# Five buffers for the last image's convolution blocks, in a kernel ordered by a planner

## The chip, the cores and the metric

The kernel runs on one core of one Trainium2 chip. The metric is the device time of one launch in microseconds (us). Five engines work side by side, each through its own instructions in order: TensorE (PE, with its weight loads shown apart as PEld), VectorE (DVE), ScalarE (ACT), GpSimd (POOL) and SyncE (SP), which here issues nearly all DMA transfers.

## The reference

Four images of 128 channels, 128 x 128 pixels, all float32, go through two residual layers.

```python
# layer 0, both halves of `_L0_conv_ref` have the same tokens and weights
x = x + block(gn(x)) + block(gn(x) transposed) transposed
#   block: t = ln0(tokens); t = t + silu(ln1(t)) @ W_out
#          w = ln2(t) @ W_whiten; k = relu(w @ W_key) ** 2
#          t = t + sigmoid(w @ W_recep) * (k @ W_value)
# layer 1
h = gn(x)
avg = h.mean(axis=(2, 3))
out = conv3x3(h, weight[0], padding=1) + bias[0]      # the gate always picks expert 0
se = sigmoid(relu(avg @ se_w1.T) @ se_w2.T)
x = x + out * se
```

The block works on each pixel (token) alone, so its transposed second half equals the first and is computed once with a factor of two. `gn` takes its mean and variance over a group of four channels of a whole image. So layer 1 of an image can't start before layer 0 of all its pixels is done: this is what shapes the end of the kernel.

## The kernel before, in words

**Work.** Layer 0 (`layer0(g)`) goes in steps `g` of 1024 pixels, 16 an image, 64 in all. A step's results are added into the block of 16 rows in a buffer with the tag `x`; after two steps the block is stored to memory (`xo`, L1100) in `spill[b]`, and statistics for the second `gn` are gathered on the way (`bx`, L1093).

Layer 1 is `conv(k, at)`, one block of 16 rows at a time, eight an image, 32 in all. It loads 18 rows (the block and a row above and below) from `spill[b]` into a buffer with the tag `xc` (L1119). The 3 x 3 convolution is computed by rows in a fast scheme that makes four rows of output from six products instead of twelve:

- VectorE forms row sums `p`, `q` (L1167, L1168) and `p2`, `q2` (L1174, L1175), tag `vt`, and from them and the rows the six inputs `v1`, `v2`, `v3`, `v4`, `v0`, `v5` (L1170, L1173, L1176, L1177, L1178 with L1179, L1180 with L1181). Their tag is `v`, with four buffers; for the last image `put` takes `h` instead, with six buffers.
- TensorE makes six products (`product(i)`, L1191 to L1193, three taps each) in the order 1, 2, 3, 4, 0, 5 with the kernels `T["uw", b, i]`, tag `uw`.
- ScalarE moves products 1 and 3 out of their banks (`e`, L1206 and L1214); VectorE forms `a`, `e1` (`ab`, L1210, L1211), `c`, `e3` (`cd`, L1218, L1219) and six operations named `y` (L1220 to L1227), which write the four output rows over rows 1 to 16 of the block's own buffer. L1225 needs product 0, L1227 product 5.
- The buffer is then stored to the output (L1237; for the last block in four parts, L1232). Only then is it free for another block's load.

Before an image's first product stands a chain of small steps, `conv_setup`: aggregate the statistics (L551), group means on TensorE (L554), variances, a root on GpSimd (L571), the squeeze-and-excite factors (L578 to L601), and the scaling of the six kernels on VectorE (L620, L626). The kernels are fetched from memory by `uw` (L633).

**Order.** Nothing is ordered by hand. Each operation is handed to a `Plan` by `op`, with its engine, an assumed cost, what it reads, writes and allocates, and a priority: the step or block it belongs to plus a number by its name from the table `SHIFT` (a low priority goes first). `Plan.order` simulates the five engines: whenever one is free it looks at the operations that are ready soonest, within `LOOK` of the first, and takes the one with the lowest priority (plus `HASTE` times its delay). `ROOM` says how many buffers each tag has; an operation that allocates is ready only when a buffer of its tag is free in the plan. The instructions are then issued in that order. So the convolution blocks of images 0 to 2 fall between the layer 0 steps of the image that follows, while the last image's eight blocks have nothing left to be mixed with. `TAIL_BANKS` gives their products six banks.

For the steps below, `x` has three buffers, `xc` two, `vt` four, `uw` nine. SP issues every load and store in plan order, and waits at the head of its queue for what the next one needs.

Of the kernel before, what the change touches and what calls it, by code (L numbers as in the profile page):

```python
# [13 lines left out]
P = 128  # L14
CH = 512
SUB = CH // P
PAIR = 2
BLK_ROWS = 16
# [2 lines left out]

BEGIN = {"ACT": 12.0, "POOL": 8.0, "PE": 8.0, "DVE": 0.5, "SP": 0.5}
SHIFT = {
    "R": -74.134, "Rc": 16.802, "Rm": -33.629, "S": 24.028, "T": -69.812, "Tz": -48.318,
    "W": -20.432, "ab": 34.928, "att": 0.537, "b": 24.437, "bn0": -1.666, "bn1": -17.948,
    "bn2": -13.51, "bx": 36.779, "c": 7.347, "cag": 14.439, "cav": -29.375, "cd": -89.85,
    "cp": -49.531, "cp1": -1.659, "cpm": -25.194, "cpr": -67.859, "cpv": -61.584, "cre": 67.032,
    "crt": -69.645, "csg": -13.711, "csp": -35.976, "cth": -17.338, "cve": 53.588, "e": 5.36,
    "e0": 16.432, "e1": -68.352, "e2": -62.698, "edge": 61.941, "fw": 14.812, "g": -11.425,
    "gag": -8.273, "gnb": -12.519, "gpm": -0.463, "gpv": -28.192, "grt": 16.489, "gsp": -8.03,  # L30
    "gve": -25.322, "in": 31.37, "in0": 114.307, "kv": 3.481, "late": 10.91, "m0": 22.359,
    "m1": -99.072, "o": -46.745, "pk": 3.203, "pq": -6.546, "pr": 2.671, "q": -82.946,
    "raw": -57.415, "rc": -6.49, "re": -98.005, "silu": -105.386, "sq": -108.331, "sqd": -40.877,
    "t": 9.446, "tD": -51.982, "tR": 23.098, "tW": -6.661, "th": -63.552, "tt": 94.047, "u": 21.426,
    "us": -20.273, "ut": 67.121, "ut2": -0.423, "uw": -43.592, "v": 45.831, "w": 114.443,
    "w0": 42.845, "w1": -39.745, "w2": -14.719, "x": 74.139, "x1": -55.714, "xc": -4.177,
    "xd": -0.904, "xf": -62.031, "xo": -5.878, "xs": -72.633, "y": 1.545, "z": 17.673, "zD": 12.117,
    "zR": 15.727, "zW": -3.804,
}
SQUARES = (("DDAA", "DDAA"), ("AAAA", "AAAA"))  # L40
TAIL_BANKS = ("Bkv", "Btr", "Btr", "Bh", "Bconv", "Bh")
CONV_AT, CONV_STEP = 2.0, 2.0
LOOK = {'PE': 0, 'DVE': 0.07, 'ACT': 0.05, 'POOL': 0, 'SP': 0.058}
HASTE = 16.739
SQUARES_AT = 17
ROOM = dict(
    x=3, xd=2, xs=2, ut=3, t=7, z=2, y=2, zd=2, zc=2, td=2, tt=2, R=2, y2=2, h=6, r=2, xc=2, vt=4, v=4,
    yt=4, uw=9, Bh=3, Bkv=1, Btr=2, Bconv=2, st=6, rs=6, nb=4, four=2, rrow=2, rd=2, zs=2, ts=2,
)
READ_AT = 3  # L50
BACKLOG = 2.189
FIRST_U_ON_DVE = (2, 3)


# [187 lines left out]
def conv_preact_kernel(  # L242
# [20 lines left out]
    nc = tc.nc  # L263
    B, C, H, W = x.shape
# [7 lines left out]
    PER = BLK // CH  # L272
# [8 lines left out]
    ps = ctx.enter_context(tc.tile_pool(name="ps", bufs=2, space=bass.MemoryType.PSUM))  # L281

    SHAPE = dict(
        x=[P, BLK_ROWS, W], xd=[P, SUB, CH], xs=[P, PAIR * CH], ut=[P, SUB, C], t=[P, SUB, C],
        z=[P, SUB, C], y=[P, CH], y2=[P, CH], h=[P, CH], r=[P, CH],
        xc=[P, BLK_ROWS + 2, W], vt=[P, Q, W], v=[P, Q, W], yt=[P, Q, W], uw=[P, 3, P],
        st=[P, N, 3], rs=[P, N], nb=[P, N], four=[P, 4, N], rrow=[P, 4 * N],
# [6 lines left out]
    T = {}  # L294

    def make(t, tag):
        pool = ps if tag[0] == "B" else sb
        T[t] = pool.tile(SHAPE[tag], F32, tag=tag, name=t[0], bufs=ROOM[tag])
        return T[t]
# [22 lines left out]
    late = []  # L322
# [51 lines left out]
    for i, (name, by) in enumerate((("g1", C**0.5), ("b1", 1.0), ("g2", C**0.5), ("b2", 1.0), ("cb", 1.0))):  # L374
        t = const.tile([P, 1], F32, tag=name, name=name)
# [4 lines left out]
    for name, row, by in (("g0", row0[0], 2 * C**0.5), ("b0", row0[1], 2.0)):  # L380
        pr = bank("prow")
        nc.tensor.matmul(pr[:, :C], ones, row, start=True, stop=True)
        t = const.tile([P, C], F32, tag=name, name=name)
# [8 lines left out]
    for src, n, dst, bias, by in ((wkt, HID, wk_s, kbias, 1.0), (wrt, P, wr_s, rbias, 0.5)):  # L392
        pw = bank("pw")
        nc.tensor.matmul(pw[:, :n], ww, src, start=True, stop=True)
        raw, raw2 = staged("raw", n), staged("raw2", HID)
# [17 lines left out]
    spill = [dram.tile([P, H, W], F32, tag=f"xo{b}", name=f"xo{b}", bufs=1) for b in range(B)]  # L413
# [5 lines left out]
    V, A, G, E, D = "DVE", "ACT", "POOL", "PE", "SP"  # L419
    TINY = (0.16, 0.2)  # L420
    READ, WRITE = (0, 0.85), (0, 0.4)

    def op(name, eng, cost, prio, emit, reads=(), writes=(), new=(), port=False, bus=0.0):
        return plan.op(name, eng, cost, prio + SHIFT.get(name, 0.0), emit, reads, writes, new, port, bus)

    def rows_of(k):
        b, kb = divmod(k, NBLK)
        return x[b, :, kb * BLK_ROWS : (kb + 1) * BLK_ROWS, :]

    def chunk_rows(t, r):  # L430
        return t[:, r :: PER, :]

    def one_input(b, i, src):
        if b not in st0:
# [300 lines left out]
    def layer0(g):  # L735
        b, p = divmod(g, NP)
        k = b * NBLK + p * PAIR // PER
        xt, xd = ("x", k), ("xd", k)
        if p * PAIR % PER == 0:

            def load():
                nc.sync.dma_start(make(xt, "x"), rows_of(k))

            op("x", D, READ, g, load, (), [(xt, r) for r in range(PER)], [(xt, "x")], bus=3.05)
            load_turned(k)
            for q in range(SUB):

                on_dve = k == 0 and q in FIRST_U_ON_DVE

                def lay(q=q, on_dve=on_dve):  # L750
                    rs, nb = gn0[b]
                    scale, bias = rs[:, q : q + 1], nb[:, q : q + 1]
                    if on_dve:
                        nc.vector.tensor_scalar(T[xd][:, q], T[xd][:, q], scale, bias, ALU.mult, ALU.add)
                    else:
                        nc.scalar.activation(T[xd][:, q], T[xd][:, q], AF.Identity, bias=bias, scale=scale)

                op(
                    "u", V if on_dve else A, (0.61, 0.7) if on_dve else (0.705, 0.82), g, lay, [(("gn0", b), 0), *((xd, a) for a in range(SUB))],
                    [(xd, ("u", q))],  # L760
                )
# [117 lines left out]
        for h in range(PAIR):  # L879
            r = (p * PAIR + h) % PER  # L880
# [11 lines left out]
        for h in range(PAIR):  # L892
            t = ("t", g, h)
# [9 lines left out]
            on, cost = (V, (0.605, 0.685)) if GAIN_ON_DVE(g) else (G, (1.232, 1.272))  # L903
# [11 lines left out]
        for h in range(PAIR):  # L915
            t, z, zt, y, att = (("t", g, h), ("z", g, h), ("zt", g, h), ("y", g, h), ("att", g, h))
# [8 lines left out]
        for h in range(PAIR):  # L925
            t, z, zt, y, att = (("t", g, h), ("z", g, h), ("zt", g, h), ("y", g, h), ("att", g, h))
            if Z_BY_DMA(g):
                zc = ("zc", g)
# [33 lines left out]
        R = ("R", g)  # L962
# [25 lines left out]
        for h in range(PAIR):  # L988
            r = (p * PAIR + h) % PER
            t, y2 = ("t", g, h), ("y2", g, h)  # L990
            if T_BY_DMA(g):
                tt = ("tt", g)
                to_channels("t", t, ("td", g), tt, h)
        for h in range(PAIR):
            r = (p * PAIR + h) % PER
            t, y2 = ("t", g, h), ("y2", g, h)
            tt = ("tt", g) if T_BY_DMA(g) else ("ttp", g, h)
# [30 lines left out]
            for j in range(NH):  # L1028
                pk, hh = ("pk", g, h, j), ("h", g, h, j)
# [24 lines left out]
            pr, gate, kv = ("pr", g, h), ("r", g, h), ("kv", g, h)  # L1054
# [41 lines left out]
        if p * PAIR % PER == PER - PAIR:  # L1096
            kb = k % NBLK

            def store():
                nc.sync.dma_start(spill[b][:, kb * BLK_ROWS : (kb + 1) * BLK_ROWS, :], T[xt])  # L1100

            op("xo", D, WRITE, g, store, [(xt, r) for r in range(PER)], [(("xo", b), kb)], bus=3.1)

# [3 lines left out]
    def conv(k, at):  # L1107
        b, kb = divmod(k, NBLK)
        ending = b == B - 1
        gn = gn1[b]  # L1110
        xc = ("xc", k)
        first, last = kb == 0, kb == NBLK - 1
        lo, hi = max(0, kb * BLK_ROWS - 1), min(H, (kb + 1) * BLK_ROWS + 1)
        shift = lo - (kb * BLK_ROWS - 1)
        n = hi - lo
        parts = ("r0", 1, 2, 3, 4, "r17")

        def load():
            nc.sync.dma_start(make(xc, "xc")[:, shift : shift + n, :], spill[b][:, lo:hi, :])  # L1119

        near = [(("xo", b), i) for i in range(max(0, kb - 1), min(NBLK, kb + 2))]
        op("xc", D, READ, at, load, [*near, (("gv1", b), 0)], [(xc, s) for s in parts], [(xc, "xc")], bus=3.4)
        for edge, row, part in ((first, 0, "r0"), (last, BLK_ROWS + 1, "r17")):
            if edge:

# [10 lines left out]
        def units(s):  # L1136
            return [(xc, p) for p in {0: ("r0", 4), 5: (1, "r17")}.get(s, (s,))]

        def name_of(n):
            return (n, k)  # L1140
# [11 lines left out]
        def do(name, eng, cost, fn, reads=(), writes=(), new=(), port=False):  # L1152
            new = [(t, "h" if tag == "v" and ending else tag) for t, tag in new]
            op(name, eng, cost, at, fn, reads, writes, new, port)
# [2 lines left out]
        TWO = (0.605, 0.685)  # L1157

        def inner(name, tag, fn, rows_in=(), tiles_in=(), extra=(), cost=TWO, inplace=False):
            t = name_of(name.rstrip("ab") if name in ("v0a", "v0b", "v5a", "v5b") else name)  # L1160
            reads = [u for s in rows_in for u in units(s)] + [(name_of(i), 0) for i in tiles_in] + list(extra)
            do(
                "v" if tag == "v" else "pq", V, cost, fn, reads + ([(t, 0)] if inplace else []), [(t, 0)],
                () if inplace else [(t, tag)], True,
            )

        inner("p", "vt", lambda: stt(put("p", "vt"), rows(2), -4.0, rows(4), ALU.mult, ALU.add), (2, 4))  # L1167
        inner("q", "vt", lambda: stt(put("q", "vt"), rows(1), -4.0, rows(3), ALU.mult, ALU.add), (1, 3))  # L1168
# [140 lines left out]
```

## Time and profile before

| what | value |
|---|---|
| median of 3 runs | 1767.89 us (1765.37 to 1768.89) |
| the profiled execution, its own time | 1767.58 us |
| its span | 1765.8 us, 18695 instructions |
| granted TensorE clock, mean | 0.995 of full speed |
| busy: PE / DVE / ACT / POOL | 1698.4 / 1421.0 / 1295.7 / 1173.4 us |
| moved by DMA | 354.66 MB, mean 201 GB/s |

How to read it: busy time is what an engine's instructions cover, matmul ends being modelled. The number in brackets at the end of a line of the timeline is the idle time just ahead of the instruction, with what ended it. A wait for several things is put down to the one that came last. A matmul in float32 appears as two records (`x2`), and three taps make one product, so a block has 36 records on PE. An SPq line is the issue of a DMA, not its transfer.

### The profile page before, as it was taken

The numbers are of one execution on the slowest core, as the hardware profiler recorded it, in microseconds if no ns is written. First come the engines' busy times: TensorE is split into PE (matmuls) and PEld (weight loads), VectorE is DVE, ScalarE is ACT, GpSimd is POOL, SyncE is SP. The second block draws the span as 40 slices with busy tenths as digits, with TensorE's granted clock in tenths as the row PEclk, the third lists the DMA queues.
The fourth block names the chain that finished last, engine by engine and source line by source line (L and its number), as shares of the span: only waits on it lengthen the run. The fifth ranks groups of instructions, "written<-read, shape, count | busy, mean of one in ns | idle before, by whom it ended". The sixth has DMA issues, their size and how long they took to land.

```text
span 1765.8 us, 18695 instructions
## 1 busy us (share of the span) xinstructions
PE 1698.4 (96%) x4870; PEld 815.2 (46%) x4870; DVE 1421.0 (80%) x2619; ACT 1295.7 (73%) x2656; POOL 1173.4 (66%) x1085
## 2 busy tenths in 40 slices
PE   5899999999999999999999999999999999998898
PEld 2444445444444444444445454444444444443343
DVE  5898788799899876879898777898988766458776
ACT  1999898998998777888878869988897865430000
POOL 1778887888897777788887858969788753210000
PEclk9999999999999999999999999999999999999999
DMA  9456666576687877767867677566777664223232
GB/s 319 131 170 209 202 195 191 171 227 222 180 259 241 244 244 231 219 224 224 271 209 259 228 251 223 189 206 197 241 222 246 202 202 139 84 76 137 107 146 97
DMA packets 140170, 354.66 MB, mean 201 GB/s; under 512 B 19079, under 2 KB 78750, under 8 KB 122782
## 3 DMA queue, kind: packets, MB, share of 16 engines
q1 hardware_dynamic: 139472, 352.99, 62.7%
q8 instruction: 39, 0.64, 0.1%
q14 instruction: 69, 0.57, 0.1%
q10 hardware_dynamic: 590, 0.46, 0.1%
HBM read 230.31 MB, written 123.07 MB: 200 GB/s over the span
## 4 chain that ended last, share of the span: by engine, by line
PE 34%; POOL 6%; DVE 5%; ACT 3%; issue 1%; DMA 1%; SPq 0%; DVEq 0%; POOLq 0%
PE kv L1070 8%; PE pk L1032 7%; PE m L1191 5%; PE m L1193 5%; PE m L1192 5%; PE pr L1057 2%; PE att L953 1%; POOL rs L819 1%; POOL four L790 1%; POOL x L1025 1%; ACT t L838 1%; POOL t L907 1%; POOL x L1085 1%; ACT h L1037 1%; POOL t L910 1%
## 5 line engine op out<-in xcount | busy, mean ns | idle before, releaser
L1070 PE MATMUL kv<-h,wv 128*128 128x512 f32 x1024 | 526.5, 598 | 9.1 <-DVE h L1049 4.2
L1032 PE MATMUL pk<-y,wk_s 128*128 128x512 f32 x1024 | 484.2, 597 | 3.2 <-ACT h L1037 2.7
L1037 ACT ACTIVATE h<-pk,kbias 128x512 f32<-128x512 f32 x512 | 335.8, 681 | 92.9 <-PE pk L1032 84.8
L1032 PEld LDWEIGHTS pk<-y,wk_s 128*128 128x128 f32 x1024 | 190.0, 190 | 237.1 <-issue 173.1
L1070 PEld LDWEIGHTS kv<-h,wv 128*128 128x128 f32 x1024 | 183.2, 190 | 215.3 <-issue 166.3
L1043 ACT ACTIVATE h<-h 128x512 f32<-128x512 f32 x444 | 267.8, 628 | 2.6
L1085 POOL TENSOR_TENSOR x<-x,r 128x512 f32<-128x512 f32 x128 | 168.4, 1316 | 145.7 <-DVE r L1079 140.5
L819 POOL TENSOR_TENSOR rs<-rs,nhalf 128x8 f32<-128x8 f32 (+1 forms) x134 | 227.0, 1697 | 40.1 <-ACT rs L816 39.9
L838 ACT ACTIVATE z<-t,nb,rs 128x128 f32<-128x128 f32 x512 | 209.5, 490 | 19.0 <-POOL nb L824 18.7
L838 ACT ACTIVATE t<-ut,nb,rs 128x128 f32<-128x128 f32 x512 | 209.4, 488 | 16.9 <-DVE st L769 9.8
L1191 PE MATMUL m<-v,uw 128*128 128x512 f32 x384 | 198.4, 598 | 14.8 <-DVE v L1170 13.7
L769 DVE BATCH_NORM_STATS2 st<-t 128x6 f32<-128x256 f32 x512 | 187.4, 411 | 20.9 <-POOL t L910 20.7
L1193 PE MATMUL m<-v,uw 128*128 128x508 f32 x384 | 196.6, 594 | 0.0
L907 POOL TENSOR_TENSOR t<-t,g 128x512 f32<-128x512 f32 x124 | 160.8, 1300 | 53.7 <-ACT t L838 53.0
L1192 PE MATMUL m<-v,uw 128*128 128x508 f32 x384 | 196.5, 593 | 0.0
L1014 POOL TENSOR_TENSOR y<-tt,R 128x512 f32<-128x512 f32 x96 | 127.4, 1331 | 74.5 <-PE pk L1032 60.6
L1025 POOL TENSOR_TENSOR x<-tt,x 128x512 f32<-128x512 f32 x124 | 163.8, 1333 | 11.5 <-DMA tt<-ts 11.1
L910 POOL TENSOR_TENSOR t<-t,b 128x512 f32<-128x512 f32 x124 | 162.0, 1315 | 2.4
L953 PEld LDWEIGHTS att<-wo,y 128*128 128x128 f32 x1024 | 130.9, 192 | 57.2 <-issue 34.7
L953 PE MATMUL att<-wo,y 128*128 128x128 f32 x1024 | 133.9, 277 | 4.2 <-ACT y L946 2.3
L1062 ACT ACTIVATE r<-pr,rbias 128x512 f32<-128x512 f32 x128 | 87.2, 681 | 67.0 <-POOL x L1085 59.6
L1079 DVE SCALAR_TENSOR_TENSOR r<-r,kv 128x512 f32<-128x512 f32 x128 | 86.9, 679 | 61.1 <-PE kv L1070 59.4
(160 smaller groups left out, 2309.7 us busy)
## 6 DMA issues: line engine op xcount, KB each, us to landing
xd<-in_x SPq DMA_DIRECT2D x128, 256.0 KB
x<-in_x SPq DMA_DIRECT2D x32, 1024.0 KB
xo<-x SPq DMA_DIRECT2D x32, 1024.0 KB
R<-rd SPq DMA_DIRECT2D x63, 512.0 KB
ts<-td SPq DMA_DIRECT2D x248, 128.0 KB
tt<-ts SPq DMA_DIRECT2D x62, 512.0 KB
out<-xc SPq DMA_DIRECT2D x31, 1024.0 KB
xc<-xo SPq DMA_DIRECT2D x24, 1152.0 KB
```

What stands on the lines that cost most here:

```text
L769: nc.vector.bn_stats(st[:, i : i + 2, :].rearrange("p n f -> p (n f)"), two)
L819: nc.gpsimd.tensor_tensor(T[rs][:, part], T[rs][:, part], nhalf[:, :k], ALU.pow)
L838: nc.scalar.activation(dst[:, s, :], src[:, s, :], AF.Identity, bias=nb[:, i : i + 1], scale=rs[:, i : i + 1])
L953: nc.tensor.matmul(pa[:, ts(m, P)], T[y][:, ts(m, P)], wo2, start=True, stop=True)
L1032: nc.tensor.matmul(make(pk, "Bh"), wk_s[:, ts(j, P)], T[y2], start=True, stop=True)
L1037: nc.scalar.activation(make(hh, "h"), T[pk], AF.Relu, bias=kbias[:, j : j + 1])
L1043: nc.scalar.activation(T[hh], T[hh], AF.Square)
L1070: nc.tensor.matmul(T[kv], wv[:, j, :], T["h", g, h, j], start=(j == 0), stop=(j == NH - 1))
L1085: nc.gpsimd.tensor_tensor(xs, xs, T[gate].rearrange("p (a w) -> p a w", a=SUB), ALU.add)
L1191: nc.tensor.matmul(pc, u[:, 1], vv, start=True, stop=False)
L1192: nc.tensor.matmul(pc[:, :, 1:W], u[:, 0], vv[:, :, 0 : W - 1], start=False, stop=False)
L1193: nc.tensor.matmul(pc[:, :, 0 : W - 1], u[:, 2], vv[:, :, 1:W], start=False, stop=True)
```

## The change

- The blocks of the last image take their buffer from `TAIL_HOMES`: blocks 0, 1, 5 and 6 from `xc` as before, blocks 2, 3, 4 and 7 from `x`, whose three buffers belong to the finished layer 0 blocks. For this `x` gets 18 rows; layer 0 uses 16 of them.
- `vt` goes from four buffers to three, `uw` from nine to eight.
- In `inner`, new dependencies named `turned` let `p`, `q`, `v1`, `v2` of block k be planned only after `v1`, `v2` of block k - 1, and the other row sums (`p2`, `q2`) after the other inputs of block k - 1; an input `v` of either kind only after all inputs of block k - 1. All of these are VectorE instructions.
- `SHIFT`, `LOOK`, `HASTE` and `BACKLOG` have new values; `hot` gets an entry of its own. They change the order of all operations.

```diff
 SHIFT = {
...
-    "W": -20.432, "ab": 34.928, "att": 0.537, "b": 24.437, "bn0": -1.666, "bn1": -17.948,
...
-    "us": -20.273, "ut": 67.121, "ut2": -0.423, "uw": -43.592, "v": 45.831, "w": 114.443,
...
-    "xd": -0.904, "xf": -62.031, "xo": -5.878, "xs": -72.633, "y": 1.545, "z": 17.673, "zD": 12.117,
...
+    "ab": 37.315, "att": 1.644, "b": 31.731, "bn0": 11.794, "bn1": -17.35, "bn2": -15.592,
+    "bx": 49.609, "c": 7.82, "cag": 6.719, "cav": -18.068, "cd": -103.804, "cp": -37.768,
...
+    "hot": -13.329, "in": 26.361, "in0": 105.375, "kv": 3.816, "late": 12.753, "m0": 23.5,
+    "m1": -101.213, "o": -54.585, "pk": 3.497, "pq": -18.954, "pr": 3.288, "q": -106.007,
...
+    "u": 16.271, "us": -19.465, "ut": 67.807, "ut2": 9.337, "uw": -50.513, "v": 57.985, "w": 117.982,
...
+    "xf": -58.371, "xo": -10.863, "xs": -54.606, "y": 24.867, "z": 15.121, "zD": 21.243,
...
 }
+TAIL_HOMES = ("xc", "xc", "x", "x", "x", "xc", "xc", "x")
-LOOK = {'PE': 0, 'DVE': 0.07, 'ACT': 0.05, 'POOL': 0, 'SP': 0.058}
-HASTE = 16.739
+LOOK = {'PE': 0.018, 'DVE': 0.087, 'ACT': 0.048, 'POOL': 0.004, 'SP': 0.048}
+HASTE = 31.975
 ROOM = dict(
-    x=3, xd=2, xs=2, ut=3, t=7, z=2, y=2, zd=2, zc=2, td=2, tt=2, R=2, y2=2, h=6, r=2, xc=2, vt=4, v=4,
-    yt=4, uw=9, Bh=3, Bkv=1, Btr=2, Bconv=2, st=6, rs=6, nb=4, four=2, rrow=2, rd=2, zs=2, ts=2,
+    x=3, xd=2, xs=2, ut=3, t=7, z=2, y=2, zd=2, zc=2, td=2, tt=2, R=2, y2=2, h=6, r=2, xc=2, vt=3, v=4,
+    yt=4, uw=8, Bh=3, Bkv=1, Btr=2, Bconv=2, st=6, rs=6, nb=4, four=2, rrow=2, rd=2, zs=2, ts=2,
 )
-BACKLOG = 2.189
+BACKLOG = 1.96
...
-        x=[P, BLK_ROWS, W], xd=[P, SUB, CH], xs=[P, PAIR * CH], ut=[P, SUB, C], t=[P, SUB, C],
+        x=[P, BLK_ROWS + 2, W], xd=[P, SUB, CH], xs=[P, PAIR * CH], ut=[P, SUB, C], t=[P, SUB, C],
...
-        return t[:, r :: PER, :]
+        return t[:, r : BLK_ROWS : PER, :]
...
-                nc.sync.dma_start(make(xt, "x"), rows_of(k))
+                nc.sync.dma_start(make(xt, "x")[:, :BLK_ROWS, :], rows_of(k))
...
+        home = TAIL_HOMES[kb] if ending else "xc"
+
         def load():
-            nc.sync.dma_start(make(xc, "xc")[:, shift : shift + n, :], spill[b][:, lo:hi, :])
+            nc.sync.dma_start(make(xc, home)[:, shift : shift + n, :], spill[b][:, lo:hi, :])
...
         def inner(name, tag, fn, rows_in=(), tiles_in=(), extra=(), cost=TWO, inplace=False):
-            t = name_of(name.rstrip("ab") if name in ("v0a", "v0b", "v5a", "v5b") else name)
+            t = name_of(name[:2] if tag == "v" else name)
             reads = [u for s in rows_in for u in units(s)] + [(name_of(i), 0) for i in tiles_in] + list(extra)
+            writes = [(t, 0)]
+            half = "12" if name in ("p", "q", "v1", "v2") else "0345"
+            if tag == "v":
+                writes += [(("turned", k, half), name)]
+                reads += [(("turned", k - 1, hf), v) for hf in HALVES for v in HALVES[hf]]
+            else:
+                reads += [(("turned", k - 1, half), v) for v in HALVES[half]]
...
+        HALVES = {"12": ("v1", "v2"), "0345": ("v3", "v4", "v0a", "v0b", "v5a", "v5b")}
```

## The prediction

> **What bounds the kernel now.** I read the page's first part, then the busy time by stretch. Columns of the second fence: stretch, its length, busy us (and instructions) of PE, PEld, DVE, ACT, POOL, then granted clock, DMA share, GB/s.
>
> ```profile
> PE 1698.4 (96%) x4870; PEld 815.2 (46%) x4870; DVE 1421.0 (80%) x2619; ACT 1295.7 (73%) x2656; POOL 1173.4 (66%) x1085
> ```
>
> ```profile
> 0.00:88.00 88.00, 60.69 (x200) 32.61 (x201) 61.28 (x121) 51.10 (x122) 38.84 (x67) 0.98 0.72 226
> 88.00:330.00 242.00, 233.60 (x777) 118.24 (x776) 205.27 (x406) 222.87 (x466) 194.71 (x189) 1.00 0.63 194
> 330.00:1590.00 1260.00, 1249.84 (x3545) 597.98 (x3544) 1018.73 (x1864) 1009.96 (x2050) 937.20 (x829) 1.00 0.67 211
> 1590.00:1766.00 176.00, 154.25 (x352) 66.34 (x350) 135.73 (x230) 11.80 (x20) 2.64 (x2) 0.97 0.32 122
> ```
>
> TensorE is the bound. Its idle time is 27.3 us in the start, 8.4 up to 330, 10.2 in the 1260 us of the middle, and 21.7 in the last 176, where the last image is convolved. Of the middle there is little to be had; the tail is where the change acts. There I asked for TensorE's waits (1597 to 1766) and for the load queue's own (1540 to 1766): us in total, times, longest.
>
> ```profile
> PE m L1191 <- DVE v L1170: 13.7, 8, 3.2
> PE cpm L554 <- DVE mv L551: 2.1, 1, 2.1
> PE m L1191 <- DVE uw L626: 0.8, 1, 0.8
> ```
>
> ```profile
> SPq L1119 <- DMA out<-xc: 32.4, 9, 4.6
> ```
>
> TensorE waits eight times for v1 (L1170), the first of a block's six inputs; and each block's load (L1119) waits for an earlier block's store, since there are two `xc` buffers. One block in order of time (start, length, what, idle before it):
>
> ```profile
> 1659.02 0.34 SPq L1237 DMA_DIRECT2D out<-xc  x1
> ...
> 1662.82 0.32 SPq L1119 DMA_DIRECT2D xc<-xo  x1
> ...
> 1665.27 0.69 DVE L1210 TENSOR_TENSOR a<-m,e 128x512 f32<-128x512 f32 x1 [1.40 <-PE m L1193]
> ...
> 1667.83 0.69 DVE L1167 SCALAR_TENSOR_TENSOR p<-xc 128x512 f32<-128x512 f32 x1 [1.15 <-DMA xc<-xo]
> ...
> 1670.39 0.69 DVE L1218 TENSOR_TENSOR c<-m,e 128x512 f32<-128x512 f32 x1 [0.67 <-PE m L1193]
> ...
> 1675.44 0.69 DVE L1227 TENSOR_TENSOR xc<-m,e 128x512 f32<-128x512 f32 x1 [0.15 <-PE m L1193]
> 1676.05 0.74 DVE L1170 SCALAR_TENSOR_TENSOR v<-p,mg,q 128x512 f32<-128x512 f32 x1
> ...
> 1676.94 1.10 PE L1191 MATMUL m<-v,uw 128*128 128x512 f32 x2 [1.53 <-DVE v L1170]
> ```
>
> Store, 3.8 us later the load, 5.0 us later p. Before that VectorE has had nothing to do twice (1.40, 1.15); afterwards it has c, e and the y's of the running block without a gap up to y4 (L1227), and v1 of the next comes behind them. TensorE ends at 1675.3 and starts at 1676.94.
>
> ```profile
> 1639.85:1659.80 19.95, 18.41 (x37) 7.84 (x37) 13.65 (x23) 1.27 (x2) 0.00 (x0) 0.86 0.29 112
> 1659.80:1745.51 85.71, 78.04 (x180) 33.78 (x181) 68.67 (x111) 6.37 (x10) 0.00 (x0) 1.00 0.34 130
> ```
>
> Five blocks in 85.71 us: 17.14 each. TensorE's need is 18 steps of 0.86, 0.85, 0.85 in the chain, 6 x 2.56 = 15.37. The difference, 1.77, is the wait of 1.53 and a first step of 1.10 for 0.86. VectorE needs 68.67 / 5 = 13.73, so it isn't the bound; its idle 3.4 us per block lie in the wrong place.
>
> [...]v1 runs at 1676.05 though p and q were done by 1669.2. [...]behind the longest wait (3.22 us, at 1639.85) the granted clock is 0.86 over the block and the first steps take 2.04, 1.69 and 1.69 us in the chain; but so do the steps at 1601 behind 2.05 us[...].[...]
>
> **The change, part by part.**
>
> *Homes.* Blocks 0, 1, 5, 6 of the last image stay in `xc`; 2, 3, 4 and 7 go to `x`. All three `x` are free soon: the last block's `xo` store is issued at 1592.11 and a store of that size took 3.8 us, so by about 1596, when the loads are first allowed (behind L551, 1598). Loads 2, 3, 4 wait for no block; 5 and 6 for the store of five blocks earlier, 7 for that of block 2. Loads of 1152 KB are a few more in flight, at a DMA share of 0.34. VectorE then finds p and q of block k+1 ready in the 1.40 gap (2 x 0.60), and p2, v1, v2 in the 1.15 + 0.67 (3 x 0.60). v1's buffer (one of six `h`) is free when product 1 of block k ends (1662.4), v2's at 1665.0. So v1 is done by about 1668.5, some 7 us before TensorE asks. VectorE's 13.73 then hides under 15.37. Gain: the six starts of blocks 2 to 7, 6 x 1.77 = **10.6 us**. If that cover fails, VectorE has 1.64 us per block before it costs time.
>
> *Start of block 1.* From 1623.55, five products should take 12.8 and block 1 came 16.3 later: 3.5 lost; block 1 took 19.95, which is 2.8 (slow clock) above the other blocks. Its load keeps `xc`, hence waits for image 2's last store (1622.86) as before; but it has landed by 1631.7 and v1 runs only at 1638.96, behind q2 and six outer operations. Between 0 and 6.3; I take **2**: q2 moves behind v1 (below), 0.6 off a wait of 3.22, and a shorter wait may spare a part of the slow steps.
>
> *Setup of the last image* (1597 to 1624): idle 2.05 + 0.31 + 0.83 + 1.24 and 1.6 of slow steps, 6.0 in all, set by statistics, kernels and the order. Three loads at about 1598 pass through SP and the DMA engines ahead of the kernel fetches; a load took 5.0 us, so from -3 to +5. I take 0.
>
> *Eight kernels for nine.* Four fetches in place of three wait for image 2's last products. The three were issued between 1604.48 and 1610.3; the fourth would follow product 4 at 1612.7. The fetch's time isn't shown; it is at most 1615.8 - 1610.3 = 5.5, so it lands by 1618.2, and the sixth scaling (L620) starts at 1618.4. 0, hidden under the chain of L554 to L601; without this cover VectorE, and behind it all outer operations, stall by what it is late, at most some 2 us.
>
> *Three row sums for four.* p, q, p2 fill them; q2 must follow v1 and v2, whose buffers wait for products. No instruction is added. In the tail it helps v1. In the middle its cover is VectorE's 19% of idle time (1018.73 busy in 1260). 0; the bad end is the second rival.
>
> *The `turned` dependencies* are between VectorE instructions only: order, no wait. Rows of `x` and slices of 16: the same bytes and shapes, 0.
>
> *New SHIFT, LOOK, HASTE, BACKLOG* reorder all engines' work. They cannot gain more than the 45.9 us of idle time outside the tail, most of it start-up; the loss has no such bound. The idle time that depends on order, 8.4 + 10.2, could move by a third: -6 to +6. I take 0.
>
> Sum: -10.6 - 2 = -12.6. The profiled execution took 1767.58 (span 1765.8 and 1.8 around it), so 1755.0; the median of the runs is 0.3 above it: **1755.3 us**. The last 4.7 us, y4 and the last stores, stay.
>
> **Rivals.**
>
> 1. *v1 stays behind y4* (0.12). The new priorities still put `v` (57.985) far behind `y` (24.867) and `cd` (-103.804): if nothing of the next block is chosen in the gaps, the wait of 1.53 stays. Against it: the planner takes what is ready first, and in the gaps nothing else is. Time 1767, plus or minus 4.
> 2. *The middle pays* (0.11), the slower side. For images 0 to 2, with four `v` buffers, q2 behind v2 makes v3 to v5 later by an operation or more (0.6), and VectorE, in order, holds the gated outputs behind it (L1079, then POOL's L1085). It decides once the 24 blocks cost TensorE (12.6 + 3.5) / 24 = 0.67 us each; at 0.8 the time is 1774.5. Against it: in 100 to 1550 no matmul waited for a v.
> 3. *The gain is given back in the setup* (0.10): loads collide with kernel fetches, +5 there, no gain at block 1: 1767.9 - 10.6 + 5 = 1762.3.
> 4. *The whole tail tightens* (0.06): block 1's 6.3 and half of the setup's 6.0 too: 10.6 + 6.3 + 3 = 19.9, 1748.
>
> **Numbers.** The likeliest has 0.61 with a range of its own of 1748 to 1761 (sum plus or minus the reorder's 6). A kernel like this can be told from no change at about 0.2%, 3.5 us. Faster: 0.59 + 0.03 + 0.09 + 0.06 and a sliver of rival 2, 0.78; same: mostly rival 1, 0.09; slower: rival 2 and a part of rival 1, 0.13. Range 1745 to 1768: above it lie rival 2 and half of rival 1, 0.16, below it some 0.03.
>
> **What would show it.** Right: seven of the last image's blocks at 15.4 to 15.6 us apart; no TensorE wait for L1170 of 1.5 us at blocks 2 to 7; v1 ahead of y4 on VectorE; no wait of p for its load; loads issued many us before their p. Middle idle within 6 us of 10.2. Wrong: blocks still 17.1 apart (rival 1), idle time of TensorE in 330 to 1590 above 20 us (rival 2), a long wait between the last `kv` and the last image's first product (rival 3). The forecast fails most easily by the reordering, which I could not price from the profile.

## The result, and the profile after

The changed kernel takes **1743.24 us** (median of 4 runs, 1740.61 to 1745.47) against 1767.65 for the kernel before: a ratio of 0.9863, interval 0.9845 to 0.988. It is faster, as forecast, but by 24.4 us instead of 12.6, and lies below the range (1745 to 1768).

The page's first part, then the busy time by stretch, for the kernel after:

```profile
PE 1690.7 (97%) x4872; PEld 815.7 (47%) x4872; DVE 1424.9 (82%) x2619; ACT 1293.8 (74%) x2656; POOL 1184.0 (68%) x1085
```

```profile
0.00:88.00 88.00, 60.06 (x198) 32.38 (x199) 62.74 (x127) 50.61 (x122) 39.95 (x68) 0.98 0.66 207
88.00:330.00 242.00, 233.50 (x773) 118.19 (x773) 206.47 (x398) 221.97 (x462) 194.80 (x187) 0.99 0.64 200
330.00:1590.00 1260.00, 1253.96 (x3570) 602.07 (x3569) 1028.13 (x1880) 1009.56 (x2054) 949.28 (x832) 1.00 0.67 213
1590.00:1741.00 151.00, 143.12 (x335) 63.08 (x333) 127.60 (x217) 11.70 (x20) 0.00 (x0) 0.99 0.32 126
```

TensorE's idle time is unchanged up to 330 (27.9 and 8.5), 6.0 for 10.2 in the middle, and 7.9 for 21.7 in the tail. TensorE's waits (1590 to 1741) and the load queue's (1540 to 1741) in the kernel after:

```profile
PE m L1203 <- DVE v L1182: 3.9, 2, 3.4
```

```profile
SPq L1122 <- DMA out<-xc: 20.5, 6, 3.5
```

Of the eight waits for v1 (now L1182) two are left, both ahead of the last image's first product. One block of the tail on VectorE, in order of time, and below it five blocks by stretch:

```profile
1679.77 0.69 DVE L1186 TENSOR_TENSOR p<-xc 128x512 f32<-128x512 f32 x1
1680.37 0.75 DVE L1182 SCALAR_TENSOR_TENSOR v<-p,mg,q 128x512 f32<-128x512 f32 x1
1681.04 0.69 DVE L1222 TENSOR_TENSOR a<-m,e 128x512 f32<-128x512 f32 x1
...
1685.87 0.69 DVE L1230 TENSOR_TENSOR c<-m,e 128x512 f32<-128x512 f32 x1 [1.15 <-PE m L1205]
...
1691.29 0.68 DVE L1239 TENSOR_TENSOR xc<-m,e 128x512 f32<-128x512 f32 x1
```

```profile
1644.62:1721.47 76.85, 76.85 (x182) 34.20 (x181) 69.22 (x115) 6.38 (x10) 0.00 (x0) 1.00 0.25 99
```

v1 of the next block stands ahead even of a and c of the running one, 11 us before y4 (now L1239), and no p waits for a load. TensorE is busy for all of 76.85 us: five blocks at 15.37, its bare need.

**Stages.** For all runs I cut the profiled execution at three matmuls: the first and the last kv (the product `k @ W_value` of layer 0, so the last one is the end of layer 0), and the first product of the last image. "Main" is from first to last kv, less 2.56 us for each product of image 2 by which fewer than eleven are left for afterwards, so that all orders stand for the same work. "Setup" is from the last kv to the last image's first product, less the products in between. "Blocks" is from there to the end of the last product. "Rest" is the start-up and the last stores. A ratio is to the kernel before as it ran beside that run, and the differences below are to that too.

| kernel | span | main (products left) | setup | blocks | rest | ratio of the runs to before |
|---|---|---|---|---|---|---|
| before | 1765.8 | 1508.9 (9) | 7.4 | 141.5 | 79.9 | |
| after | 1740.9 | 1502.2 (11) | 6.0 | 124.5 | 80.0 | 0.9863 (0.9845 to 0.988) |
| e1_all_xc | 1751.7 | 1501.6 (11) | 6.0 | 134.5 | 81.4 | 0.9917 (0.9888 to 0.9947) |
| e2_room | 1787.1 | 1533.3 (8) | 8.9 | 138.8 | 77.9 | 1.0116 (1.008 to 1.0152) |
| e3_homes | 1780.1 | 1535.3 (8) | 13.0 | 125.0 | 78.6 | 1.0087 (1.006 to 1.0115) |
| e4_numbers | 1771.6 | 1520.3 (11) | 9.5 | 137.2 | 76.4 | 1.0065 (1.0044 to 1.0087) |
| e5_old_numbers | 1779.2 | 1534.2 (8) | 13.0 | 125.0 | 78.8 | 1.009 (1.0063 to 1.0118) |
| e6_uw8 | 1761.0 | 1505.7 (9) | 7.4 | 138.7 | 81.1 | 0.9995 (0.9979 to 1.0012) |
| e7_x_first | 1739.0 | 1504.6 (11) | 5.6 | 124.8 | 75.8 | 0.9851 (0.9826 to 0.9877) |
| e8_backlog | 1765.3 | 1529.9 (11) | 6.0 | 125.9 | 75.3 | 1.002 (1.001 to 1.0029) |
| e9_three | 1742.0 | 1503.0 (11) | 6.0 | 124.8 | 80.0 | 0.9863 (0.9831 to 0.9894) |
| e10_kv | 1750.3 | 1504.6 (8) | 11.5 | 125.6 | 80.4 | 0.9924 (0.9895 to 0.9953) |
| e11_before_look | 1775.4 | 1524.7 (9) | 7.1 | 140.4 | 75.0 | 1.0075 (1.0047 to 1.0104) |
| e12_early | 1740.8 | 1505.8 (11) | 3.4 | 123.0 | 80.4 | 0.9841 (0.9814 to 0.9868) |

Before to after, the 24.9 us of the span are 17.0 in the blocks, 6.7 in the main part and 1.4 in the setup, with 0.1 the other way in the rest and rounding. After, e1, e7, e9 and e12 have the same order on every engine up to the setup; their main parts lie between 1501.6 and 1505.8 and their rests between 75.8 and 81.4, so a difference of some 4 us in the main part, or 6 in the rest, is that of one execution from another.

### The profile page after: what moved, and what is told of

It reads as the page before. It is cut to its first block, busy times and chain, and to the rows that moved or that the text cites. A ratio compares the mean times of both kernels' runs of the same rounds, so it can differ in the third digit from the quotient of the medians.

```text
span 1740.9 us, 18709 instructions
## 1 busy us (share of the span) xinstructions
PE 1690.7 (97%) x4872; PEld 815.7 (47%) x4872; DVE 1424.9 (82%) x2619; ACT 1293.8 (74%) x2656; POOL 1184.0 (68%) x1085
## 4 chain that ended last, share of the span: by engine, by line
PE 71%; ACT 10%; POOL 8%; DVE 7%; DMA 2%; issue 2%; SPq 0%; ACTq 0%; DVEq 0%; POOLq 0%
PE kv L1071 19%; PE pk L1033 18%; PE m L1203 7%; PE m L1204 7%; PE m L1205 7%; PE att L954 5%; PE pr L1058 5%; ACT t L839 2%; ACT h L1038 2%; POOL rs L820 2%; ACT z L839 2%; DVE st L770 1%; ACT h L1044 1%; POOL x L1026 1%; POOL t L908 1%
## 5 line engine op out<-in xcount | busy, mean ns | idle before, releaser
L1015 POOL TENSOR_TENSOR y<-tt,R 128x512 f32<-128x512 f32 x96 | 130.9, 1367 | 59.8 <-PE pk L1033 46.9
L1058 PE MATMUL pr<-y,wr_s 128*128 128x512 f32 x256 | 132.3, 600 | 3.9 <-ACT h L1038 3.0
```

Of the source, the lines that this page charges most:

```text
L1058: nc.tensor.matmul(make(pr, "Bh"), wr_s, T[y2], start=True, stop=True)
```

## The experiments

Theory 1: the buffers take away the wait at the blocks' starts, the order does the rest. Theory 2: the new numbers alone put v1 early. Theory 3: three row sums force q2 behind v1. The homes weren't tried quite alone: the longer `x` takes 3 KB more a partition (three buffers, two rows of 512 bytes each), for which three `vt` and eight `uw` give up 2 and 1.5 KB, and without `turned` the planner finds no order for them. So the homes are undone in the changed kernel (e1), and put on top of a kernel that already has the smaller room (e2 to e3).

**e1_all_xc: the changed kernel without the homes.**

```diff
-TAIL_HOMES = ("xc", "xc", "x", "x", "x", "xc", "xc", "x")
+TAIL_HOMES = ("xc",) * 8
```

> The changed kernel, with the last image's eight blocks back in the two xc buffers. The order of all engines is then that of the changed kernel up to the last image's setup. Theory 1 (the buffers remove the wait at each block's start, some 17 us in the tail; the reordering gives the other 7 before it): 1754 to 1760 us, blocks of the last image about 17 us apart, TensorE waiting for v1 at most block starts. Theory 2 (the new numbers, not the buffers, put v1 early): 1743 to 1747, blocks 15.4 apart.

1751.84 us, 8.6 more than the changed kernel; by stages all of it in the blocks, 134.5 for 124.5. Theory 2 falls. But it is also less than theory 1's 1754 to 1760: from the third on, the blocks stand 15.45, 18.02, 17.0, 18.02 and 15.45 us apart (the 17.0 is 15.45 with slow steps behind a wait; the granted clock is 0.98 over 1630 to 1720), not 17.14. TensorE's waits from 1600 on, and p of one block on VectorE:

```profile
PE m L1203 <- DVE v L1182: 9.9, 4, 2.5
```

```profile
1656.19 0.69 DVE L1179 SCALAR_TENSOR_TENSOR p<-xc 128x512 f32<-128x512 f32 x1 [1.01 <-DMA xc<-xo]
...
1659.49 0.74 DVE L1182 SCALAR_TENSOR_TENSOR v<-p,mg,q 128x512 f32<-128x512 f32 x1
```

With two buffers the load is late again, but every second block's v1 gets in ahead of e3 and the y's.

**e2_room: the smaller room with the old numbers**, and **e3_homes: the homes on top of it.** Both have `turned` for the last image's blocks alone.

```diff
-    ... vt=4, v=4, yt=4, uw=9, ...
+    ... vt=3, v=4, yt=4, uw=8, ...
```

> The kernel before with three vt, eight uw and the turned dependencies for the last image alone; old numbers, two xc buffers. Theory 1: 1764 to 1771, no gain. Theory 3 (the smaller room forces q2 behind v1 and so v1 ahead of the outer operations, which is most of the gain): 1750 to 1758. The second rival of the prediction (the middle pays for three vt): 1771 or more, with over 4 us more idle time of TensorE between 330 and 1590.

> The kernel of the run before this one (three vt, eight uw, turned for the last image, old numbers) with the five buffers of the change. Against it, theory 1: 10 to 17 us faster, so 1750 to 1757 if that one is at 1767, blocks 2 to 7 at 15.4 us. Theory 2: less than 4 us faster, blocks still near 17.

e2 takes 1785.61, 20 us more than before: neither theory 1 nor 3, but what the prediction's second rival feared, if by another mechanism. From the third on its blocks stand 18.02 and 15.45 apart in turn, 16.7 on average of the two, so in this room too every second v1 slips ahead, worth 0.4 us a block. The loss is in the main part, 24.4 us, and most of it in one place. The stretch from 550 to 650 in the kernel before and in e2, and e2's TensorE there:

```profile
550.00:650.00 100.00, 100.00 (x293) 48.83 (x292) 82.69 (x154) 79.35 (x166) 77.96 (x68) 1.00 0.80 252
```

```profile
550.00:650.00 100.00, 83.97 (x226) 39.60 (x225) 84.58 (x149) 63.53 (x137) 74.43 (x65) 0.95 0.71 223
```

```profile
571.88 2.04 PE L1202 MATMUL m<-v,uw 128*128 128x512 f32 x2 [9.10 <-DVE v L1192]
...
598.96 3.33 PE L953 MATMUL att<-wo,y 128*128 128x128 f32 x14 [4.31 <-ACT y L933]
```

From 562 to 600 there is no key or value matmul at all: the layer 0 steps in flight run dry at once, TensorE has convolution products and some of the small `att` matmuls, and waits 9.1 us for an input of one product. In the same 38 us of the kernel before TensorE has no idle time.

e3 takes 1780.37, 5 us less than e2 (the intervals of the two ratios overlap); theory 1 expected 10 to 17. The blocks do what it says: 13.8 us less, 15.37 apart from the second on. But the setup takes 4.1 more, in one wait (TensorE's waits from 1600 on):

```profile
PE m L1205 <- DVE v L1184: 6.1, 1, 6.1
```

This is the size of the third rival's +5, gain given back ahead of the first product, but not its mechanism, a collision of loads. In e3's order on VectorE no operation there waits for a load, and v1 of block 0 comes straight behind image 2's last outer operations (`ab`, `cd` and `y`):

```profile
1649.48 0.67 DVE L1239 TENSOR_TENSOR xc<-m,c 128x512 f32<-128x512 f32 x1
1650.08 0.74 DVE L1184 SCALAR_TENSOR_TENSOR v<-p,mg,q 128x512 f32<-128x512 f32 x1
```

**e4_numbers: the new numbers alone**, in the old room, with two buffers.

```diff
 SHIFT = {
...
-HASTE = 16.739
+HASTE = 31.975
...
-BACKLOG = 2.189
+BACKLOG = 1.96
```

> The kernel before with the new SHIFT, LOOK, HASTE and BACKLOG alone: two xc buffers, four vt, nine uw, no turned dependencies. Theory 1: about 7 us faster than before, 1757 to 1764, all of it ahead of the last image's first product. Theory 2: 1743 to 1750. If the order's effect is a matter of chance (the planner answers to any small change with another order), anything from 1758 to 1774.

1777.55, 12 us slower than before: the main part is 11.4 longer, the blocks stand at 17.14. Neither theory has this; the remark on chance was the nearest.

**e5_old_numbers: the changed kernel with the old numbers** (the same diff the other way).

> The changed kernel with the old SHIFT, LOOK, HASTE and BACKLOG: five buffers, three vt, eight uw, turned for all blocks. Theory A (the new numbers are fitted to the smaller room, and the loss ahead of the tail belongs to old numbers in that room): 1774 to 1786 us, blocks 15.4 apart in the tail all the same. Theory B (turned for all blocks is what repairs the order ahead of the tail): 1748 to 1760.

1781.57, as theory A had it. Its order is that of e3 on every engine, and its stages are those of e3 within 1.1 us: `turned` for all blocks does nothing with the old numbers. So the new numbers are worth some 38 us in the new room, and cost 12 in the old one.

**e6_uw8: eight kernels alone.**

```diff
-    yt=4, uw=9, ...
+    yt=4, uw=8, ...
```

> The kernel before with eight kernel buffers for nine, nothing else. If the kernels are what breaks the plan near 570 us with the old numbers: 1778 to 1790, some 20 us of lost TensorE time in one place. If it is the row sums, or chance: 1763 to 1772. The prediction had 0 to 2 us for this edit.

1763.26, no difference from before: the kernels aren't what breaks e2's order. That leaves the three row sums, alone or together with the eight kernels; with old numbers and nine kernels the planner gets stuck over three row sums, so they weren't tried alone. (`turned`, the rest of e2's edit, is there for the last image alone, 1000 us later.) The run shows something else. Its tail has the waits of the kernel before to a tenth, and yet its blocks take 2.8 us less. Waits of e6, then the wait at block 1 in the kernel before and in e6:

```profile
PE m L1191 <- DVE v L1170: 13.7, 8, 3.2
```

```profile
1639.85 2.04 PE L1191 MATMUL m<-v,uw 128*128 128x512 f32 x2 [3.22 <-DVE v L1170]
```

```profile
1638.66 1.10 PE L1191 MATMUL m<-v,uw 128*128 128x512 f32 x2 [3.22 <-DVE v L1170]
```

The same 3.22 us of idling stood ahead of a first step of 2.04 us in one execution and of 1.10 in the other; the last section has the granted clocks.

**e7_x_first and e12_early: what is left ahead of block 0.** e12 has e7's homes, and in addition:

```diff
-TAIL_HOMES = ("xc", "xc", "x", "x", "x", "xc", "xc", "x")
+TAIL_HOMES = ("x", "x", "x", "xc", "xc", "x", "x", "x")
...
-                "v" if tag == "v" else "pq", V, cost, fn, reads + ([(t, 0)] if inplace else []), writes,
+                ("early" if ending and kb == 0 else "v") if tag == "v" else "pq", V, cost, fn, reads + ([(t, 0)] if inplace else []), writes,
```

> The changed kernel with the homes x, x, x, xc, xc, x, x, x: blocks 0 to 2 load as soon as layer 0 is done. If TensorE's wait of 3.42 us and the slow steps ahead of the last image's first product come from block 0's load behind image 2's store: 3 to 6 us faster than the changed kernel, 1737 to 1740. If they come from VectorE's order (v1 behind image 2's outer operations): 1742 to 1745.

> The homes of the run x, x, x, xc, xc, x, x, x, and the inputs v of the last image's first block under a priority name of their own that SHIFT lacks, so that they stand ahead of image 2's last outer operations on VectorE; GpSimd and SP in the same order as there, all engines the same ahead of the setup. If what is left of TensorE's wait ahead of block 0 (2.09 us and two to three us of slow steps) is VectorE's order: 2 to 4 us faster than that run, 1734 to 1737, and the first block 15.4 us long. If the outer operations then come late for block 1: no gain, 1737 to 1741.

e7 took 1738.38, as the first case had it, but not for its reason: setup and blocks are 130.4 us together, those of the changed kernel 130.5. Its profile is shorter in the rest, which changes from execution to execution, and the intervals of the two ratios overlap. The wait is still there; TensorE, then VectorE in e7:

```profile
1610.15 1.89 PE L1203 MATMUL m<-v,uw 128*128 128x512 f32 x2 [2.09 <-DVE v L1182]
```

```profile
1608.76 0.68 DVE L1239 TENSOR_TENSOR xc<-m,e 128x512 f32<-128x512 f32 x1
1609.36 0.74 DVE L1182 SCALAR_TENSOR_TENSOR v<-p,mg,q 128x512 f32<-128x512 f32 x1
```

v1 comes straight behind image 2's last outer operation, as the second case said. In e12 it stands ahead of those: setup and blocks are 126.4, 4.0 less, all eight blocks 15.37 apart, and TensorE's waits from 1580 on are

```profile
PE m L1203 <- ACT e L1226: 0.7, 1, 0.7
PE m L1203 <- DVE v L1182: 0.4, 1, 0.4
```

Of the whole time nothing of it can be told: 1737.48, ratio 0.9841 with an interval that overlaps e7's and the changed kernel's; its profiled execution had 1.2 more in the main part than e7's and 4.6 more in the rest, in an order that is the same up to the setup.

**e8_backlog and e10_kv: orders drawn beside the changed kernel's; e11_before_look: one beside that of before.**

```diff
-BACKLOG = 1.96
+BACKLOG = 2.0
```

```diff
-    "kv": 3.816,
+    "kv": 4.0,
```

```diff
-LOOK = {'PE': 0, 'DVE': 0.07, ...
+LOOK = {'PE': 0, 'DVE': 0.075, ...
```

> The changed kernel with BACKLOG 2.0 for 1.96, which alters nothing but the order drawn. If the 5.7 us gained ahead of the tail are a property of the new numbers at large: 1741 to 1746. If they are one order out of many that lie some us apart: 1746 to 1760, with the last image's blocks still 15.4 apart.

> The changed kernel with 4.0 for 3.816 as the number of kv, a second order drawn beside it. If the last run's 1769.7 was a rare bad order: 1741 to 1748. If the changed kernel's own order is the rare good one: 1750 to 1775. Blocks of the last image 15.4 apart in both.

> The kernel before with LOOK 0.075 for 0.07 on VectorE: an order drawn beside the one of before. If its order too was a picked one: 1775 to 1795, lost ahead of the tail, with the last image's blocks still about 17 us apart. If orders lie close together on this side: 1763 to 1772.

1769.67, 1751.53 and 1777.67. A step of 2 per cent in one number of the planner costs the changed kernel 26 us, one of 5 per cent in another 8, and one of 7 per cent in a third costs the kernel before 10. In e8 and e11 the loss is in the main part (27.7 and 15.8), in e10 in the setup (5.5), with 2.4 in the main part. From 250 to 400, the changed kernel and e8:

```profile
250.00:400.00 150.00, 143.05 (x475) 72.61 (x474) 123.49 (x240) 132.41 (x276) 120.30 (x115) 0.99 0.59 185
```

```profile
250.00:400.00 150.00, 136.15 (x435) 67.15 (x433) 115.03 (x220) 119.78 (x247) 107.69 (x104) 0.97 0.54 174
```

All engines do less there, so no one of them is the bound; I read it as the layer 0 steps out of step, as in e2 (the longest stretch without a kv is 26.7 us in e8, from 382 on, and 10.6 in the changed kernel). Part of e8's loss goes with a lower clock: the granted one is 0.97 from 250 to 400 and 0.97 from 400 to 550, where the changed kernel has 0.99 and 1.00. The last image's blocks stay 15.37 apart from the second on in e8 and e10, and at 17.14 from the third on in e11.

**e9_three: how many buffers it takes.**

```diff
-TAIL_HOMES = ("xc", "xc", "x", "x", "x", "xc", "xc", "x")
+TAIL_HOMES = ("xc", "xc", "x", "xc", "xc", "x", "xc", "xc")
```

> The changed kernel with the homes xc, xc, x, xc, xc, x, xc, xc: in effect three buffers, each block's load waiting for the store of three blocks before. Store 3.8, load 5.0 and p, q, v1 some 2 us are 10.8 of a block's 15.37, so if one buffer more than before is all the tail needs: blocks 15.4 apart, 1741 to 1746. If VectorE needs more lead: blocks 16 or more apart, 1748 to 1754.

1741.64, the changed kernel's time; blocks 15.37 apart from the second on. Blocks 3, 4, 6 and 7 were loaded behind the store of three blocks before, and that is early enough. Block 5 was not: `x` has a buffer to spare, and its load was issued together with block 2's:

```profile
1582.11 0.92 SPq L1122 DMA_DIRECT2D xc<-xo  x2
```

So this run held four buffers, not "in effect three". That one buffer more than before is enough follows for block 5 from its likeness to the others, and wasn't run.

## Why the prediction was right or wrong

*Homes, 10.6 us: right.* The six starts of blocks 2 to 7 lost 1.77 each, and all are gone, in every order that has the buffers (after, e3, e5, e7 to e10, e12). The mechanism is as predicted: p no longer waits for its load, v1 runs in VectorE's gaps ahead of y4, VectorE's work (69.22 / 5 = 13.84 us a block) fits under 15.37. Undoing the homes alone costs 10.0 in the blocks, 1.6 of it slow steps of that execution. The first rival (v1 stays behind y4) fell.

*Start of block 1, "I take 2": mis-sized.* The first two blocks took 40.3 us before and 32.25 after, 8.1 less, of which 1.8 was counted with the homes. Of the other 6.3, 3.5 is the wait ahead of block 1, 1.5 a wait inside block 0 that the prediction had under the setup (its 1.24), and 1.3 slow steps: 2.8 before (granted clock 0.86 over block 1's 19.95 us), 1.5 after (0.92 over block 0's 16.88). That the sum is the upper end of the prediction's "between 0 and 6.3" is luck, since the parts are others. The step took 0.6 off the wait, for q2 alone. In the changed kernel v1 of block 1 went ahead of e3 and the y's of block 0 too, 4.2 us before TensorE asks for it, and the wait is gone:

```profile
1624.39 0.69 DVE L1230 TENSOR_TENSOR c<-m,e 128x512 f32<-128x512 f32 x1 [1.90 <-PE m L1205]
1625.00 0.74 DVE L1182 SCALAR_TENSOR_TENSOR v<-p,mg,q 128x512 f32<-128x512 f32 x1
```

Its load keeps `xc`, but it comes earlier as well, since the new order has image 2's last outer operations ahead of block 0's first product:

```profile
1611.68 0.34 SPq L1249 DMA_DIRECT2D out<-xc  x1
1615.54 0.32 SPq L1122 DMA_DIRECT2D xc<-xo  x1
```

```profile
1612.37 2.07 PE L1203 MATMUL m<-v,uw 128*128 128x512 f32 x2 [3.42 <-DVE v L1182]
```

The load is issued 3.2 us behind block 0's first product, where it was 7.2 (1626.71 against 1619.48). Block 1 starts without a wait in e1, which lacks the buffers, and in e3 and e5, which lack the new numbers; e2, which lacks both, still waits 2.6 us there. So either will do in the smaller room. And the 2.8 of slow steps before are missing in e6 with the same wait: I took one execution's accident for a part of the kernel.

*Setup, 0: inside its range of -3 to +5, mis-sized.* 1.4 gained up to the first product, 2.9 with the 1.5 above, which the prediction had counted here. That this is the planner's draw too is seen in e3, e5 and e10, where it costs 4.1 to 5.6 more than before. The third rival's sign, a long wait ahead of the first product, is there (3.42 us, above), but the setup is none the longer.

*Eight kernels, 0: right in the old order* (e6). In the new one VectorE does stand for a fetch in the setup, which the prediction had as the bad case; whether a ninth buffer would have spared it wasn't run:

```profile
1603.69 0.62 DVE L621 SCALAR_TENSOR_TENSOR uw<-uw,rs,row 128x384 f32<-128x384 f32 x1 [1.12 <-DMA uw<-raw]
```

*`turned`, order without a wait: right* (e3 against e5), though without it there is no plan.

*Three row sums, 0 in the middle: right for the changed kernel, wrong with the old numbers*, where the smaller room costs 24.4 us in the main part (e2). The second rival had the place and not the form: not 0.67 us at each of 24 blocks, but one stretch in which layer 0 runs dry.

*New SHIFT, LOOK, HASTE, BACKLOG, "-6 to +6, I take 0": the step that failed.* Against the spans of the two profiles the forecast was missing some 12.3 us: 6.7 in the main part, 4.3 at the start of the blocks, 1.4 in the setup. All three came with another order of the same operations, which the sum had at nothing but for the 2 at block 1. How much of the 6.7 belongs to the order is not settled: the five executions of the changed order have a main part of 1503.4 on average, 5.5 below the one of before; that of e6 is 3.2 below it, with a plan of the same length; and TensorE's idle time in the middle fell by 4.2. So this change may have stayed inside the range there. But the range was wrong in its idea: I took the idle time of the one order I saw as what any order could move. The orders run here have main parts from 1502 to 1535 us. With the old numbers the whole change would have been slower than before (e5, 1.009); with one number off by 2 per cent, no faster (e8, 1.002).

What lets layer 0 run dry stays open, and I don't see it in the profile of before. But the profile wasn't the only source: the planner's simulation gives each operation a start (`Plan.timed`) when the program is built, and the prediction uses none of them. Cut in the same way, these starts give a main part of 1474.6 us for the kernel before, 1473.5 after, 1482.5 in e4, 1485.1 in e11, 1489.3 in e8 and 1491.2 in e2, e3 and e5: each loss against before is there, at about two thirds of what was measured, and the changed order has none. They also have the last image's blocks 20.1 and then 16.9 us apart before, and 15.4 after.

## What to carry to other kernels

Where the same unit works through a buffer that must be stored before it is loaded again, add up store, load and first operations (here 3.8 + 5.0 + 2) against the period (15.4): if the engine that feeds the bound has idle time while it waits and a full queue afterwards, more buffers turn that time into lead. Here a load behind the store of three blocks before was early enough (e9), and the fifth buffer added nothing to that. When a change comes with new constants for a greedy planner, the constants are a change of their own: read the times of the planner's own simulation first, run it with them a little off before any of its gain is put down to the buffers, and compare by stage, since the tail's 10 us were as predicted while the rest moved by 30.

## What the runs showed of the hardware

The length of a wait alone didn't tell whether slow steps followed it. The first steps behind six of TensorE's waits, and the granted clock of four:

| run | wait, us | at | next steps, us | granted clock |
|---|---|---|---|---|
| before | 3.22 | 1639.85 | 2.04, 1.90, 1.90 | 0.50 over 1638.68 to 1645.51 |
| e6_uw8 | 3.22 | 1638.66 | 1.10, 1.01, 1.01 | 1.00 over 1634.5 to 1654.8 |
| after | 3.42 | 1612.37 | 2.07, 1.52, 1.02 | 0.50 over 1611.82 to 1615.23 |
| e7_x_first | 2.09 | 1610.15 | 1.89, 1.90, 1.15 | |
| e3_homes | 6.10 | 1650.87 | 2.08, 1.90, 1.24 | |
| before | 1.53 | 1676.94 | 1.10, 1.01, 1.01 | 1.00 over 1659.80 to 1745.51 |

So 3.22 us came with slow steps once and without them once, and 2.09 us came with them. What tells these apart is open. A stretch that stands behind such a wait should be priced with and without slow steps, some 3 us here (2.8 in the kernel before, none in e6).

And start-up with the last stores took between 75.8 and 81.4 us in five profiled executions that issue the start-up in the same order, more than the 3.5 us that I took for the measure of no change.
